# A graph network of four layers on one core: bf16 sums of weights in the first part of the last attention head, and one-time sums cut at the border of the head's parts

## The chip, the cores and the metric

The kernel runs on one core of a Trainium2 chip. The metric is the device time of that core in microseconds (us): the median of several executions. Times inside the kernel come from one further execution that the hardware profiler recorded.

## The reference

A graph of 2708 nodes has 512 features a node (`x`) and a symmetric 0/1 matrix `adj` with ones on the diagonal. Four layers are applied one after another, each as `x = x + L_i(relu(layernorm(x)), adj)`. L0 is a graph convolution, L1 a mean over the first 64 neighbours with two linear maps, L2 attention, L3 a sum over neighbours with two linear maps. The change lies in L2, which has 8 heads of 64 columns. For one head:

```python
Wh = h @ W[head]                       # 2708 x 64
e = leaky_relu(f1 + f2.T, 0.2)         # f1 = Wh @ a1, f2 = Wh @ a2: a number for each pair of nodes
att = softmax(where(adj > 0, e, -9e15), axis=1)
out = elu(att @ Wh)
```

## The kernel before, in words

**The trick of L2.** exp(leaky_relu(f1 + f2)) is the larger of two products, each of a factor of the row and a factor of the column. The kernel takes one factor out on each side, so that a tile of weights is the maximum of a row `rb` (the exponential of a row of numbers, the same in all partitions) and a number per partition `ec`, times the adjacency pattern `vT` of those nodes. The other number per partition, `ef`, is multiplied into the right operand. The softmax's denominator is the sum of the weights over the neighbours.

**Tiles and stages.** The neighbours (partitions) are cut into NC = 22 chunks of R = 126 nodes, the last of 62. The nodes that receive (columns) are whole, 2708 wide, for heads 1 to 6. For head 0 and head 7 they are cut in two parts at `cut` = 1384: units (lines 803 to 805) are head 0's two parts, heads 1 to 6, head 7's two parts: u = 0 to 9. Each unit has 22 steps, one per chunk (line 807), so there are 220 steps.

**One step.** `scale` (line 868, ScalarE) makes `whs`: the chunk's 64 columns of Wh times `ef` (line 874), and, where the sums need it, a block `one6` with a single column of ones times `ef` (line 876). `make` (line 880, VectorE, line 886) makes the tile of weights `t`, in one of four buffers. `multiply` (line 1077, TensorE) calls `four` (line 1065), whose matmuls (line 1069) each fill one of four groups of 32 columns of the array: `av`, the products of the weights with Wh in fp32, in pieces of the columns' halves, and `sums`, the weights' sums in fp32, in pieces of the columns' quarters. A part of 1384 columns has two pieces of 346 for `av` and one for `sums`; a whole head has three of some 451 and two of 338 and 339.

**Sums by side.** For some steps the fp32 pass for `sums` is replaced. `compare` (line 897, ScalarE, line 904) makes a 0/1 pattern `b` in bf16 that says for which neighbours the maximum was the row's number (a very steep sigmoid with the threshold in `eb`). `multiply_sides` (line 1092) multiplies this pattern in bf16 with `parts`, the factors split in three bf16 parts each, whose columns add up in the same PSUM buffers as the `sums` do. What does not depend on the pattern `b`, the sum over all neighbours of a factor of the partition, is the same for all such steps and is counted once at the start: `mask` (line 1138, ScalarE, line 1143) copies the adjacency of a chunk to bf16, a quarter of the columns at a time (677), and `count_neighbors` (line 1145, TensorE, line 1155) multiplies it with `parts2`, the split factors of all heads concerned, and after the last chunk stores the result to `sumT`. `split` (line 1117) makes `parts` and, with one copy (line 1132), `parts2`. Which steps go by side: chunks m with m mod 5 in 1, 3, 4, 13 of the 22 (BY_SIDE, line 795), in heads 1 to 6 (`by_side`, lines 809 and 810).

**What sets the order.** Each engine executes its instructions in the order in which the program issues them. The main loop (lines 1224 to 1239) issues for step s: the load of Wh for step s+6, scaling and making for s+3, comparing for s+1, multiplying for s, multiplying by side for s-1, and then what a plan holds for this step (`behind`, from line 1182): the split at step 9, the masks and the counting from step 11, the weights of layer 3 and `er` at step 30, evictions (`evict`, line 1102) at the end of each unit, the first steps of layer 3 in the last ones. In the built program some instructions stand elsewhere than in this loop, since a scheduler places them.

**Memory.** The pool `weights` (line 120) has two buffers of 8 KB a partition that all layers' weight matrices share, in order of use. The rows `a1` and `a2` lie in a pool of their own (line 915, loaded by `load_row`, line 176) and are read by `product2` (line 919). The pool `e3` (line 993) holds `er`, `rest` (scratch of `split`, and declared in line 995) and later `b3`, the bias of layer 3 (line 1246), which `self3` (line 1258) adds in line 1263. When `e3` is closed, the pool of layer 3's casts takes its place: `weight3` (line 1294) casts the pattern to `kt` in line 1296, for the matmuls in line 368. `load_l3_weights` (line 1177) loads `wfs` and `wfn`, layer 3's matrices.

Of the kernel before, what the change touches and what calls it, by code (L numbers as in the profile page):

```python
# [8 lines left out]
F32 = mybir.dt.float32  # L9
F32R = mybir.dt.float32r  # L10
BF16 = mybir.dt.bfloat16
# [9 lines left out]
P = 128  # L21

R = 126
# [21 lines left out]
def fast_layers(  # L45
# [36 lines left out]
    nc = tc.nc  # L82
    N, D = x_in.shape
    H, _, O = w2.shape
    NC = -(-N // R)
    NF = D // P
# [5 lines left out]
    def rows(c):  # L92
        return min(R, N - c * R)
# [26 lines left out]
    weights = ctx.enter_context(tc.tile_pool(name="weights", bufs=2))  # L120
    dram = ctx.enter_context(tc.tile_pool(name="dram", bufs=1, space=DRAM))

    common = ctx.enter_context(tc.tile_pool(name="common", bufs=2))

    ps = ctx.enter_context(tc.tile_pool(name="ps", bufs=8, space=PSUM, reuse_waits="tile"))
# [47 lines left out]
            nc.sync.dma_start(w[:, i], src[i * P : (i + 1) * P, :])  # L173
        return w

    def load_row(pool, src, name, tag=None):

        t = pool.tile([P, D], F32, name=name, tag=tag or name)
        nc.sync.dma_start(t, bass.AP(tensor=src.tensor, offset=src.offset, ap=[[0, P], [1, D]]))
        return t  # L180

# [107 lines left out]
    with tc.tile_pool(name="pre", bufs=2) as pre:  # L289
        ws = [load_weight(pre, w_self, "ws")]  # L290
        wc = load_weight(pre, w_comb, "wc", k=2 * NF)
        ws.append(load_weight(pre, w_nb3, "ws"))
        bc = load_row(pre, b_comb, "bc")
        bcol = pre.tile([P, 2 * NF], F32, name="bcol")
        for i, b in enumerate((b_self, b_nb3)):
# [51 lines left out]
    vT = []  # L347
# [69 lines left out]
    with ExitStack() as ring_ctx:  # L417
        ring = ring_ctx.enter_context(tc.tile_pool(name="ring", bufs=NC - 1, side="right"))
# [29 lines left out]
        with tc.tile_pool(name="l0", bufs=2) as wk:  # L448
            units = [(g, m) for g in range(len(groups)) for m in range(NC)]
# [191 lines left out]

        wk = ring_ctx.enter_context(tc.tile_pool(name="l1", bufs=1, side="right"))
        bl = load_row(wk, b_line1, "bl")
        bn = load_row(wk, b_nb1, "bn")
        wn, wl = l1_weights
        h1, turned = {}, {}
# [148 lines left out]
    BY_SIDE = [m for m in range(NC) if m % 5 in (1, 3, 4)]  # L795
# [6 lines left out]
    cut = EARLY * R // 8 * 8  # L802
    units = [(h, 0, N) for h in range(H)]
# [3 lines left out]
    steps = [(u, m) for u in range(len(units)) for m in range(NC)]  # L807

    def by_side(u, m):
        return 0 < units[u][0] < H - 1 and m in BY_SIDE  # L810

    whd = dram.tile([N, D], F32, name="whd")
    avT = dram.tile([D, N], F32, name="avT")
# [2 lines left out]
    sumT = dram.tile([NS, N], F32, name="sumT")  # L816
# [4 lines left out]
    at = at_ctx.enter_context(tc.tile_pool(name="att", bufs=1, reuse_waits="tile"))  # L821
# [3 lines left out]
    parts = at.tile([R, NC * H * 8 + S], BF16, name="parts")  # L825
    nc.gpsimd.memset(parts, 0.0)
    parts_of = parts[:, : NC * H * 8].rearrange("p (m h k) -> p m h k", h=H, k=8)
    parts2 = at.tile([R, NC, H, 3], BF16, name="parts2")
    nc.gpsimd.memset(parts2, 0.0)
    one6 = at.tile([R, S], F32, name="one6")  # L830
    nc.gpsimd.memset(one6, 0.0)
# [36 lines left out]
    def scale(s):  # L868

        u, m = steps[s]  # L870
        h, q = units[u][0], rows(m)
        t = at.tile([R, O + S], F32, name="whs", bufs=4)
        by = ef[:q, m, h : h + 1]
        ins = nc.scalar.activation(t[:q, :O], wh.pop((u, m))[:q], AF.Copy, scale=by)  # L874
        if not by_side(u, m):
            nc.scalar.activation(t[:q, O:], one6[:q], AF.Copy, scale=by)
        whs[s] = t
        scaled.append(ins.ins)
# [18 lines left out]
    def compare(s):  # L897

        u, m = steps[s]
        h, lo, hi = units[u]  # L900
        q = rows(m)
        if by_side(u, m):
            b = at.tile([R, N], BF16, name="b", bufs=2)
            nc.scalar.activation(  # L904
                b[:q, : hi - lo],
                weight[s][:q, : hi - lo],
                AF.Sigmoid,
                bias=eb[:q, m, h : h + 1],
                scale=STEEP,
            )  # L910
            sides[s] = b

    l2p = ctx.enter_context(ExitStack())
    pp = l2p.enter_context(tc.tile_pool(name="l2p", bufs=2, side="right", reuse_waits="tile"))
    ar = [load_row(pp, a, f"arow{i}") for i, a in enumerate((a1, a2))]

    products, firsts = {}, {}

# [73 lines left out]
    e3_ctx = ctx.enter_context(ExitStack())  # L992
    e3 = e3_ctx.enter_context(tc.tile_pool(name="e3", bufs=2, side="right", reuse_waits="tile"))
    er = e3.tile([R, NC, H], F32, name="er", bufs=1)
    rest = e3.tile([R, NC, H], F32, name="rest", bufs=1)
    kept3, l3_weights = {}, []


# [56 lines left out]
    def pieces(w):  # L1055

        k = -(-w // 512)
        cuts = [round(i * w / k) for i in range(k + 1)]
        return list(zip(cuts, cuts[1:]))
# [57 lines left out]
    def split():  # L1117

        nc.scalar.mul(eb, ec, -STEEP * ABOVE)
        for i in range(2):  # L1120
            e = ef
            if i:
                nc.vector.tensor_tensor(rest, ec, ef, ALU.mult)
                e = rest
            for k in range(3):
                part = parts_of[:, :, :, 3 * i + k]
                nc.scalar.copy(part, e)
                if k < 2:
                    nc.vector.tensor_tensor(rest, e, part, ALU.subtract)
                    e = rest  # L1130
        heads = slice(1, H - 1)
        nc.scalar.copy(parts2[:, :, heads], parts_of[:, :, heads, 3:6])


    quarter = N // 4
    counted, masks = [], {}

    def mask(i, j):
        m = BY_SIDE[i]
        q = rows(m)  # L1140
        g, k = where[m]
        t = masks[i, j] = common.tile([P, D], F32, name="x", bufs=XBUFS).bitcast(BF16)
        nc.scalar.copy(t[:q, :quarter], vT[g][:q, k, j * quarter : (j + 1) * quarter])

    def count_neighbors(i):
        m = BY_SIDE[i]
        q = rows(m)
        if i == 0:
            counted.extend(
                ps.tile([P, 512], F32, name="adj_sums", tag="ps") for _ in pieces(quarter)  # L1150
            )
        w = parts2[:q, m].rearrange("p h k -> p (h k)")
        for p, (a, b) in zip(counted, pieces(quarter)):
            for j in range(4):
                nc.tensor.matmul(
                    p[j * S : j * S + 3 * H, : b - a],
                    w,
                    masks[i, j][:q, a:b],
                    start=(i == 0),
                    stop=(i == len(BY_SIDE) - 1),  # L1160
                )
        if i < len(BY_SIDE) - 1:
            return
        for p, (a, b) in zip(counted, pieces(quarter)):
            t = common.tile([P, D], F32, name="out", tag="t", bufs=3)
            for j in range(4):
                own = slice(j * S, j * S + 3 * H)
                nc.scalar.copy(t[own, : b - a], p[own, : b - a])
                nc.sync.dma_start(
                    sumT[7 * H :, j * quarter + a : j * quarter + b], t[own, : b - a]  # L1170
                )

    def exp_nodes():
# [16 lines left out]
    behind(5, load_row1, *units[1])  # L1190
    behind(6, exp_row, *units[1])
    behind(9, split)
    behind(30, load_l3_weights)
    behind(30, exp_nodes)
# [8 lines left out]
    for i in range(len(BY_SIDE)):  # L1203
        for j in range(4):
            behind(11 + 2 * i + j // 2, mask, i, j)
        behind(13 + 2 * i, count_neighbors, i)
# [17 lines left out]
    for s in range(len(steps)):  # L1224
        if s + 6 < len(steps) and (s + 6) % NC % GROUP == 0:
            load_wh(s + 6)
        if s + 3 < len(steps):
            scale(s + 3)
            make(s + 3)
        if s + 1 < len(steps):  # L1230
            compare(s + 1)
        multiply(s)
        multiply_sides(s - 1)
        for fn, args in plan.pop(s, ()):
            if fn in (load_l3_weights, exp_nodes, split):
                with tc.issue_after(made[s]):
                    fn(*args)
            else:
                fn(*args)
# [3 lines left out]

    with ExitStack() as stack:
        ring = stack.enter_context(tc.tile_pool(name="ring3", bufs=NC - 1, reuse_waits="tile"))
        b3 = e3.tile([P, D], F32, name="b3", bufs=1)
        nc.sync.dma_start(
            b3, bass.AP(tensor=bias3.tensor, offset=bias3.offset, ap=[[0, P], [1, D]])
        )
# [688 lines left out]
def kernel(tc: tile.TileContext, *args: bass.AP):  # L1938

    nc = tc.nc  # L1940
    with tc.tile_pool(name="verdict", bufs=1) as pool:
        verdict = pool.tile([1, 1], I32, name="verdict")
        fast_layers(tc, *args, verdict)
        odd = nc.values_load(verdict[0:1, 0:1], min_val=0, max_val=P + 1)
        with tc.If(odd > 0):
            general_layers(tc, *args)
# [32 lines left out]
```

## Time and profile before

| | us |
|---|---|
| median of 3 runs | 1822.22 |
| lowest, highest | 1820.46, 1822.46 |
| profiled execution | 1820.7 |
| its span | 1818.8 |
| TensorE busy in it | 1781.6 |
| VectorE busy | 1307.9 |
| ScalarE busy | 798.0 |
| all matmuls of line 1069, `av` | 436.2 |
| all fp32 matmuls of line 1069, `sums` | 139.6 |

The profile gives for each engine its busy time, the groups of instructions by line with the mean duration of one, and what ended the idle time before them. The chain of waits follows the work that ended last back to its start; it says which engine sets the time in a stretch. A timeline lists what an engine did, with equal instructions in a row joined (x16 is sixteen of them). PE is TensorE, DVE is VectorE, ACT is ScalarE, POOL is GpSimd, SP is SyncE, which only issues transfers. The mean TensorE clock granted over the span was 0.996 of full speed. Attention's steps run from about 853 to 1411 us, unit 8 from 1330.5 to 1369, and layer 3's sum over the neighbours from 1589.7.

### The profile page before, as it was taken

The numbers are of one execution on the slowest core, as the hardware profiler recorded it, in microseconds if no ns is written. First come the engines' busy times: TensorE is split into PE (matmuls) and PEld (weight loads), VectorE is DVE, ScalarE is ACT, GpSimd is POOL, SyncE is SP. The second block draws the span as 40 slices with busy tenths as digits, with TensorE's granted clock in tenths as the row PEclk, the third lists the DMA queues.
The fourth block names the chain that finished last, engine by engine and source line by source line (L and its number), as shares of the span: only waits on it lengthen the run. The fifth ranks groups of instructions, "written<-read, shape, count | busy, mean of one in ns | idle before, by whom it ended". The sixth has DMA issues, their size and how long they took to land.

```text
span 1818.8 us, 30698 instructions
## 1 busy us (share of the span) xinstructions
PE 1781.6 (98%) x11884; PEld 1036.1 (57%) x11884; DVE 1307.9 (72%) x1836; ACT 798.0 (44%) x1542; POOL 245.3 (13%) x241
## 2 busy tenths in 40 slices
PE   9899999999999999999999999999999999999998
PEld 4456777654447887644444344444444454488776
DVE  4942998955546655888999999999998777533334
ACT  2642777722110000156887767767744566400000
POOL 0101333301121111266000000000001222100000
PEclk9999999999999999999999999999999999999999
DMA  7632666635461211343221121122022444313221
GB/s 248 193 114 67 204 208 196 204 76 121 117 149 55 67 54 46 97 147 104 73 61 26 42 62 43 27 61 57 13 65 56 134 131 139 94 38 102 78 69 45
DMA packets 165554, 176.63 MB, mean 97 GB/s; under 512 B 94830, under 2 KB 115792, under 8 KB 164516
## 3 DMA queue, kind: packets, MB, share of 16 engines
q1 hardware_dynamic: 143170, 131.47, 26.2%
q10 hardware_dynamic: 18484, 33.28, 5.4%
q0 software_dynamic: 3744, 9.82, 1.6%
q8 instruction: 96, 1.57, 0.4%
q14 instruction: 60, 0.49, 0.1%
HBM read 111.35 MB, written 55.15 MB: 92 GB/s over the span
## 4 chain that ended last, share of the span: by engine, by line
PE 80%; DVE 9%; issue 4%; DMA 4%; ACT 1%; POOL 1%; SPq 0%; DVEq 0%; ACTq 0%; POOLq 0%
PE acc L368 31%; PE av L1069 19%; PE nb_ps L184 7%; PE sums L1069 6%; PE self_ps L184 4%; PE wh_ps L184 3%; DVE t L886 3%; PE line_ps L184 3%; DVE cum L494 2%; PE h_ps L184 2%; PE hT_ps L212 2%; PE fused_ps L312 2%; DMA x<-x 1%; DMA ai<-in_adj 1%; DVE two L506 1%
## 5 line engine op out<-in xcount | busy, mean ns | idle before, releaser
L886 DVE SCALAR_TENSOR_TENSOR t<-rb,ec,vT 126x2708 f32<-126x2708 f32 (+2 forms) x220 | 532.2, 2472 | 17.6 <-PE sums L1069 9.7
L368 PE MATMUL acc<-halves,kt 126*126 126x512 f32 x1848 | 435.9, 395 | 3.9 <-DVE kt L741 2.3
L1069 PE MATMUL av<-t,whs 126*32 126x451 f32 (+3 forms) x4576 | 436.2, 515 | 0.6 <-DVE ln_mv L191 0.6
L368 PEld LDWEIGHTS acc<-halves,kt 126*126 126x126 f32 x1848 | 342.6, 186 | 93.7 <-DVE kt L741 6.9
L1069 PEld LDWEIGHTS av<-t,whs 126*32 126x32 f32 (+1 forms) x4576 | 158.7, 110 | 207.8 <-issue 188.0
L368 PE MATMUL acc<-halves,ar 126*126 126x512 f32 x924 | 232.7, 405 | 2.1 <-DVE deg L502 1.1
L904 ACT ACTIVATE b<-t,eb 126x2708 bf16<-126x2708 f32 (+1 forms) x78 | 199.1, 2552 | 25.4 <-DVE t L886 25.1
L368 PEld LDWEIGHTS acc<-halves,ar 126*126 126x126 f32 x924 | 169.1, 186 | 52.7 <-issue 7.7
L193 ACT ACTIVATE ln_rs<-ln_mv,eps 126x1 f32<-126x1 f32 x88 | 25.6, 293 | 339.5 <-DVE ln_mv L191 336.5
L741 DVE SCALAR_TENSOR_TENSOR kt<-lastr,index,vT 126x504 fp32r<-126x504 int16 (+3 forms) x154 | 110.6, 729 | 81.0 <-PE acc L368 80.7
L1296 DVE CAST kt<-vT 126x504 fp32r<-126x504 uint8 (+3 forms) x154 | 56.0, 366 | 138.2 <-PE acc L368 138.2
L1069 PE MATMUL sums<-t,whs 126*32 126x338 f32 (+5 forms) x1568 | 139.6, 449 | 2.4 <-ACT out L1110 2.4
L874 ACT ACTIVATE whs<-wh,ef 126x64 f32<-126x64 f32 x220 | 76.8, 349 | 130.6 <-PE sums L1069 66.1
L1036 POOL TENSOR_SCALAR z<-y 126x512 f32<-126x512 f32 x22 | 44.0, 2000 | 662.2 <-DVE y L1029 653.4
L494 DVE TENSOR_TENSOR_SCAN cum<-ai,deg 126x504 int16<-126x504 int32 (+2 forms) x110 | 128.6, 1182 | 0.5 <-DMA ai<-in_adj 0.5
L522 ACT ACTIVATE cum<-cum,limit 126x504 int16<-126x504 int16 (+3 forms) x132 | 88.2, 668 | 58.4 <-DVE deg L502 57.3
L1069 PEld LDWEIGHTS sums<-t,whs 126*32 126x32 f32 (+1 forms) x1568 | 54.9, 109 | 70.0 <-issue 43.7
L189 DVE BATCH_NORM_STATS2 ln_st<-x 126x6 f32<-126x512 f32 x88 | 60.4, 686 | 43.1 <-DMA x<-x 29.1
L184 PE MATMUL h_ps<-w0s,hT 128*126 128x512 f32 x176 | 79.7, 596 | 6.0 <-ACT hT L214 4.7
L184 PE MATMUL nb_ps<-wfn,hT 128*126 128x512 f32 x176 | 81.7, 608 | 2.0 <-ACT hT L214 2.0
L184 PE MATMUL wh_ps<-w2s,hT 128*126 128x512 f32 (+1 forms) x176 | 79.4, 593 | 0.0
L184 PE MATMUL nb_ps<-wn,hT 128*126 128x512 f32 x176 | 79.2, 592 | 0.0
(182 smaller groups left out, 1869.8 us busy)
## 6 DMA issues: line engine op xcount, KB each, us to landing
x<-x SPq DMA_DIRECT2D x105, 252.0 KB
x<-x ACTq DMA_DIRECT2D x84, 252.0 KB
ai<-in_adj SPq DMA_DIRECT2D x84, 249.0 KB
x<-in_x SPq DMA_DIRECT2D x42, 252.0 KB
rb<-rT SPq DMA_DIRECT2D x7, 1332.8 KB
wh<-whd SPq DMA_DIRECT2D x70, 94.5 KB
packed<-two POOLq DMA_DIRECT2D x44, 124.5 KB, 4.3
whd<-wh SPq DMA_DIRECT2D x21, 252.0 KB
```

The lines of the kernel that those rows point to most:

```text
L184: nc.tensor.matmul(po[:n], lhsT[:, f, :n], w[:, f, :], start=(f == 0), stop=(f == NF - 1))
L189: nc.vector.bn_stats(st[:n], xc[:n])
L368: nc.tensor.matmul(acc[:R], weight[:, k * R : (k + 1) * R], parts[:, i, :], start=(m == 0 and i == 0), stop=(m == NC - 1),)
L494: nc.vector.tensor_tensor_scan(cum[:n, :gw], ai[:n, :gw], ai[:n, :gw], 0.0 if g == 0 else deg[:n, m : m + 1], op0=ALU.add, op1=ALU.max,)
L522: nc.scalar.activation(cum[:n, :gw], cum[:n, :gw], AF.Sign, bias=limit[:n], scale=-1.0, accum_out=signs[:n, m, g : g + 1],)
L741: nc.vector.scalar_tensor_tensor(by_chunk(kt, cs), lastr[:, cs[0] * R : (cs[-1] + 1) * R].rearrange("p (c r) -> p c r", r=R), index[:R, m ...
L874: ins = nc.scalar.activation(t[:q, :O], wh.pop((u, m))[:q], AF.Copy, scale=by)
L886: ins = nc.vector.scalar_tensor_tensor(t[:q, : hi - lo], row[h][:q, lo:hi], ec[:q, m, h : h + 1], vT[g][:q, k, lo:hi], op0=ALU.max, op1=AL ...
L904: nc.scalar.activation(b[:q, : hi - lo], weight[s][:q, : hi - lo], AF.Sigmoid, bias=eb[:q, m, h : h + 1], scale=STEEP,)
L1036: nc.gpsimd.tensor_scalar(z, y, 0.0, None, op0=ALU.min)
L1069: nc.tensor.matmul(p[j * S : (j + 1) * S, : b - a], lhsT, rhs[:, part * size + a : part * size + b], start=(s % NC == 0), stop=(s % NC == ...
L1296: nc.vector.tensor_copy(by_chunk(kt, cs), pattern(m, cs))
```

## The change

1. `by_side` takes unit 8, head 7's first part, in too. Its 13 steps of BY_SIDE get a comparison and a bf16 pass in place of a scaling of `one6` and an fp32 pass.
2. The one-time sums are cut at 0, 692, 1384, 2046 and 2708 instead of in quarters of 677, so that no piece crosses the border between head 7's parts. `parts2` holds two sets of factors for each of the 13 chunks: with head 7 for the first two fourths, without it for the others. `split` fills it with six copies instead of one.
3. Three things move in memory: the rows `a1` and `a2` into a buffer of the pool `weights`, `rest` to the pool `common`, `b3` to the pool `ring3`.

```diff
     def by_side(u, m):
-        return 0 < units[u][0] < H - 1 and m in BY_SIDE
+        return 1 < u < len(units) - 1 and m in BY_SIDE
...
-    parts2 = at.tile([R, NC, H, 3], BF16, name="parts2")
+    parts2 = at.tile([R, len(BY_SIDE), 2, H, 3], BF16, name="parts2")
...
-    ar = [load_row(pp, a, f"arow{i}") for i, a in enumerate((a1, a2))]
+    arows = weights.tile([P, NF, D], F32, name="arows", tag="w")
+    ar = [load_row(None, a, None, into=arows[:, i]) for i, a in enumerate((a1, a2))]
...
-    rest = e3.tile([R, NC, H], F32, name="rest", bufs=1)
...
     def split():
...
+        rest = common.tile([P, D], F32, name="rest", tag="t", bufs=3)
+        rest = rest[:R, : NC * H].rearrange("p (m h) -> p m h", h=H)
...
-        heads = slice(1, H - 1)
-        nc.scalar.copy(parts2[:, :, heads], parts_of[:, :, heads, 3:6])
-    quarter = N // 4
+        for i, heads in enumerate((slice(1, H), slice(1, H - 1))):
+            for r in sorted({m % 5 for m in BY_SIDE}):
+                ms = [m for m in BY_SIDE if m % 5 == r]
+                src = parts_of[:, r :: 5, heads, 3:6]
+                at_i = [BY_SIDE.index(m) for m in ms]
+                nc.scalar.copy(parts2[:, at_i[0] : at_i[-1] + 1 : 3, i, heads], src)
+    fourths = [0, cut // 2, cut, (cut + N) // 2, N]
...
-        nc.scalar.copy(t[:q, :quarter], vT[g][:q, k, j * quarter : (j + 1) * quarter])
+        nc.scalar.copy(t[:q, : own.stop - own.start], vT[g][:q, k, own])
...
-        for p, (a, b) in zip(counted, pieces(quarter)):
+        for n, p in enumerate(counted):
             for j in range(4):
+                a, b = pieces_of(j)[n]
                 nc.tensor.matmul(
                     p[j * S : j * S + 3 * H, : b - a],
-                    w,
+                    parts2[:q, i, j // 2].rearrange("p h k -> p (h k)"),
                     masks[i, j][:q, a:b],
...
-        b3 = e3.tile([P, D], F32, name="b3", bufs=1)
+        b3 = ring.tile([P, D], F32, name="b3", bufs=1)
```

In the order of instructions of the changed program, beside the above: on SP's queue the two rows are loaded where `wfs` was, `wfs` where `wfn` was, `wfn` behind it and one load of `wh`, and `b3` behind the last stores of the sums; on VectorE the first three casts of line 1296 stand ahead of the last normalization and the last three additions of line 1263, behind which they stood before. The comparison for the second step of unit 8 stands on ScalarE ahead of unit 7's evictions.

More of the change, by code (lines that the diff above doesn't have):

```diff
@@ L174, in load_weight, with load_row @@
         return w
-    def load_row(pool, src, name, tag=None):
-        t = pool.tile([P, D], F32, name=name, tag=tag or name)
+    def load_row(pool, src, name, into=None):
+        t = into
+        if t is None:
+            t = pool.tile([P, D], F32, name=name)
         nc.sync.dma_start(t, bass.AP(tensor=src.tensor, offset=src.offset, ap=[[0, P], [1, D]]))
@@ L1130, in split, with pieces_of @@
                     e = rest
-        heads = slice(1, H - 1)
-        nc.scalar.copy(parts2[:, :, heads], parts_of[:, :, heads, 3:6])
-    quarter = N // 4
+        for i, heads in enumerate((slice(1, H), slice(1, H - 1))):
[5 more added lines that the diff above has]
+    fourths = [0, cut // 2, cut, (cut + N) // 2, N]
     counted, masks = [], {}
+    def pieces_of(j):
+        return pieces(fourths[j + 1] - fourths[j])
     def mask(i, j):
@@ L1141, in mask @@
         g, k = where[m]
+        own = slice(fourths[j], fourths[j + 1])
         t = masks[i, j] = common.tile([P, D], F32, name="x", bufs=XBUFS).bitcast(BF16)
-        nc.scalar.copy(t[:q, :quarter], vT[g][:q, k, j * quarter : (j + 1) * quarter])
+        nc.scalar.copy(t[:q, : own.stop - own.start], vT[g][:q, k, own])
     def count_neighbors(i):
@@ L1149, in count_neighbors @@
             counted.extend(
-                ps.tile([P, 512], F32, name="adj_sums", tag="ps") for _ in pieces(quarter)
+                ps.tile([P, 512], F32, name="adj_sums", tag="ps") for _ in pieces_of(0)
             )
-        w = parts2[:q, m].rearrange("p h k -> p (h k)")
-        for p, (a, b) in zip(counted, pieces(quarter)):
+        for n, p in enumerate(counted):
             for j in range(4):
+                a, b = pieces_of(j)[n]
                 nc.tensor.matmul(
                     p[j * S : j * S + 3 * H, : b - a],
-                    w,
+                    parts2[:q, i, j // 2].rearrange("p h k -> p (h k)"),
                     masks[i, j][:q, a:b],
@@ L1163, in count_neighbors @@
             return
-        for p, (a, b) in zip(counted, pieces(quarter)):
+        for n, p in enumerate(counted):
             t = common.tile([P, D], F32, name="out", tag="t", bufs=3)
             for j in range(4):
+                a, b = pieces_of(j)[n]
                 own = slice(j * S, j * S + 3 * H)
@@ L1169, in count_neighbors @@
                 nc.sync.dma_start(
-                    sumT[7 * H :, j * quarter + a : j * quarter + b], t[own, : b - a]
+                    sumT[7 * H :, fourths[j] + a : fourths[j] + b], t[own, : b - a]
                 )
```

## The prediction

> **What bounds the kernel now.** I read the busy shares first, then the chain of work that ended last, then the timelines of TensorE, VectorE and ScalarE in the stretches that the edits touch.
>
> ```profile
> PE 1781.6 (98%) x11884; PEld 1036.1 (57%) x11884; DVE 1307.9 (72%) x1836; ACT 798.0 (44%) x1542; POOL 245.3 (13%) x241
> PE 80%; DVE 9%; issue 4%; DMA 4%; ACT 1%; POOL 1%; SPq 0%; DVEq 0%; ACTq 0%; POOLq 0%
> ```
>
> TensorE (PE) is busy 98% of the span and is 80% of the chain. A microsecond of matmul taken out is a microsecond won, unless the next engine in that stage is late. So I look at the stage: unit 8, head 7's first part, from 1330.5 to 1369 us. The chain of waits there holds nothing but PE (start, us, what):
>
> ```profile
> 1334.56 1.17 PE av L1069 x16
> 1335.72 0.58 PE sums L1069 x8
> 1336.31 1.17 PE av L1069 x16
> 1337.47 0.58 PE sums L1069 x8
> ```
>
> A step is 1.17 + 0.58 = 1.75 us (the starts of `av` are 1.75 apart). `av` is two pieces of 346 columns by four column groups in fp32, `sums` one such piece. The groups show what is to take the place of `sums`, and what the other engines would have to deliver (busy us, mean ns of one, idle before):
>
> ```profile
> L1069 PE MATMUL sums<-t,whs 126*32 126x346 f32 x336 | 32.1, 453 | 0.0
> L1069 PE MATMUL sums<-b,parts 126*32 126x338 bf16 x288 | 25.0, 306 | 0.0
> L886 DVE SCALAR_TENSOR_TENSOR t<-rb,ec,vT 126x1384 f32<-126x1384 f32 x42 | 69.1, 1659 | 7.8 <-ACT rb L849 2.6 <-PE sums L1069 2.5 <-PE av L1069 1.1
> L904 ACT ACTIVATE b<-t,eb 126x2708 bf16<-126x2708 f32 x72 | 183.7, 2552 | 23.6 <-DVE t L886 23.2 <-ACT whs L874 0.2
> ```
>
> The mean ns of a matmul includes its pipeline and overlaps its neighbours' (453 against 306 understates the difference), so I take starts. In a whole head, a bf16 pass has two pieces, of 338 and 339 columns, and moves the next `av` by 0.29 us (1311.16 to 1311.45, in the timeline). One piece of 346 is then 0.146 x 346/338.5 = 0.15 us.
>
> VectorE is idle only about 0.1 us in each step: it waits for a buffer that PE releases (four buffers of `t`). ScalarE rests in most of each step (start, us, in brackets the idle before):
>
> ```profile
> 1339.91 0.35 ACT L874 ACTIVATE whs<-wh,ef 126x64 f32<-126x64 f32 x1 [1.18 <-issue]
> 1340.17 0.31 ACT L876 ACTIVATE whs<-one,ef 126x32 f32<-126x32 f32 x1
> 1341.67 0.35 ACT L874 ACTIVATE whs<-wh,ef 126x64 f32<-126x64 f32 x1 [1.20 <-PE sums L1069]
> ```
>
> Two other places matter. At the start of layer 3's sum over neighbours PE stands 1.39 us for a cast that VectorE does behind the last `y`:
>
> ```profile
> 1589.73 2.55 PE L368 MATMUL acc<-halves,kt 126*126 126x512 f32 x10 [1.39 <-DVE kt L1296]
> 1588.37 0.68 DVE L1263 TENSOR_TENSOR y<-self_ps,b 62x512 f32<-62x512 f32 x1 [2.12 <-PE self_ps L184]
> 1589.17 1.07 DVE L1296 CAST kt<-vT 126x504 fp32r<-126x504 uint8 x3
> ```
>
> And at the end of attention PE idles 0.60 and 1.83 us, and then runs at half clock for two windows (1409.65 to 1416.48):
>
> ```profile
> 1407.71 0.62 PE L212 MATMUL hT_ps<-ident,hn 126*128 126x126 f32 x4 [1.83 <-DVE hn L203]
> 1411.63 6.09 PE L184 MATMUL nb_ps<-wfn,hT 128*126 128x512 f32 x8
> ```
>
> **What the Trainium skill says.** "FP8 and Floating Point Precision", section TensorE Precision Notes: true fp32 takes four passes through the array. The trace agrees: 0.58 us against 0.15 is a ratio of 3.9. "ScalarE: Activation LUTs", section What ACT_TABLE_LOAD costs: an activation with a per-partition bias takes about 280 ns plus 0.833 ns an element, whatever the function; L904 at 2708 columns would be 2.54, and 2.552 was measured. "TensorE: Matmul & The Clock Gate", section What's actually happening: too little work in a window of 3413 ns halves the clock, and the window runs free. The trace has just such windows at 1409.65. "DMA: Bandwidth & Descriptors", section Issuing engines are not separate DMA queues: loads of all queues share the same 16 engines. So moved loads must be looked at for what they land beside.
>
> **The change, part by part.**
>
> *Unit 8's sums.* 13 of its 22 steps (m mod 5 in 1, 3, 4) lose the fp32 pass (0.58) and get a bf16 one (0.15), one step later in PE's order: 13 x 0.43 = 5.6 us less on PE. Unit 8 goes from 22 x 1.75 = 38.5 to 9 x 1.75 + 13 x 1.32 = 32.9. Can the others follow?
> - VectorE must make 22 tiles. One has a duration of 1.66, but in a run where it waits for nothing they start 1.57 apart (1321.78, 1323.35): 34.5 us, 1.6 more than PE. It enters unit 8 with its four buffers full: a tile is ready about 3.3 us before PE takes it. 3.3 - 1.6 leaves 1.7 at the end (1.3 when I step through the order with the buffer releases). Unit 9 stays as it is (PE 1.68, VectorE 1.51 a step), so the lead grows back by 0.17 a step. If tiles came 1.66 apart, VectorE would need 36.5, 0.3 us more than PE and lead together; counting release delays I put the gain then at 3.8.
> - ScalarE gets 13 compares in place of 13 scalings of `one6` (0.31 each). The trace has no compare of 1384 columns. Bounds: 1.36, the exponential of that width on the same engine (next of kin, without a bias operand), and 2.55, a whole-width compare. I take 1.43: 0.28 + 0.833 x 1.384 by the page, and 2.552 less 1324 columns at 0.836 (the slope of L849 from 1384 to 2708) is 1.44. Work in unit 8, without waits: 9 x 0.56 + 13 x (0.25 + 1.43 - 0.09 of overlap) + 2.4 for unit 7's evictions = 28.1 (9.5 + 13 compares), under PE's 32.9. It would reach 32.9 at a compare of 1.80 and 38.5 at 2.23.
> - The compare stands ahead of unit 7's evictions (`out<-av`), which then come up to 1.4 us later. Units 7 and 8 together hold 5 + 3 of the eight PSUM buffers, and unit 9 needs its own only 30 us on: free.
> - The unseen cost is the bf16 pass in steps this short: 0.15 at best, 0.30 (a whole pass's time) at worst: gain 5.6 to 3.6. I take 5.6.
>
> *One-time sums in fourths.* 104 mask copies keep their total width (692 + 692 + 662 + 662 = 2708), 104 matmuls too: 26 pieces are wider by some 8 columns, below 0.1 us each way. One copy of `parts2` (0.54) becomes six of 84 to 105 elements, each about the 0.25 to 0.29 of L876: some 1.1 us more on ScalarE between 876.8 and 880.6, where it idles 0.34 + 1.19 us. Cost 0; if that cover is gone, PE waits up to 1 us more for the masks, for which it already waits 0.9 us in all. The memset on GpSimd grows from 528 to 624 elements, far ahead of its use.
>
> *Moved buffers and loads.* The two `a` rows go into a weight buffer, so on SP's queue they take the place of `wfs` at 545 us, `wfs` takes that of `wfn` (from 853.8), and `wfn`, 1 MB, comes behind it, waiting for the last product that reads the rows (about 856.5, before SP arrives there). Behind these four on SP stand `er` and the group of `wh` issued at 864.1, which is needed at 868.4. At 0.82 us an issue, `wfn` takes SP from 858.2 to 861.5 and lands by about 864, since 1 MB takes near 4 us at the 277 GB/s seen here: a slack of some 2 us stays. Cost 0; up to 2 us if it were used up. `b3` no longer lies in the buffer pool of `rest` and `er`; its load goes from 858.3 to behind the last sums' stores, at 1414 in the times of before, ahead of the next `aT`, `sT` and `x`. It is first read at 1422.0, 8 us later; the page gives 4.3 us to landing for a load of half its size, so some 3 us are left. Cost 0, at worst 1.
>
> *Layer 3's first casts.* As `b3` left that pool, the pool's next owner, `kt`, no longer waits for the last reader of `b3`. VectorE's order in the changed program has the first three casts before the last norm and the last three `y`. VectorE has idle stretches of 0.8 to 3.4 us there, and the delayed norm has 4 us of slack. The 1.39 us go; next late is nothing, since `halves` are ready.
>
> Sum: -5.6 - 1.4 + 0.1 = -6.9 us on the profiled execution's 1820.7: 1813.8. The median is 1822.2, 1.5 more, and I move it alike: **1815.3**.
>
> **The rivals.**
> 1. *VectorE or the short pass sets unit 8's pace in part*: -3.7 - 1.4, 1817.1. For it: VectorE's total is above PE's. Against it: the lead.
> 2. *The casts' wait is replaced*, by the next operand or by a colder clock: -5.6 alone, 1816.7. PE's clock and the last `y` there speak for it.
> 3. *The windows at the end of attention move.* Half clock for 6.8 us costs about 3.5 us; the earlier end gives another phase. Both ways alike: 1811.8 or 1818.8.
> 4. *Unit 8 doesn't get faster at all*, VectorE being held by its buffers, which now wait for ScalarE's reading too: -1.4, 1820.8.
> 5. *Slower: ScalarE becomes the bound of unit 8.* If the compare does not shrink with its width (2.55), ScalarE needs 9.5 + 13 x 2.55 = 42.7 against 38.5 before, and 13 waits from engine to engine, of the 0.1 us that VectorE shows, make it 44.0: +5.5 - 1.4 = +4.1, 1826.3. It costs from 2.23 us a compare on, and outweighs the casts' 1.4 from 2.34. Against it: the exponential of 1384 columns took 1.36.
>
> **How the numbers follow.** Chances: my forecast 0.54 (1813.3 to 1817.3); rival 1 0.12; rival 2 0.11; rival 3 0.05 each way; rival 4 0.07; rival 5 0.06. A measurement of this kernel can tell some 0.2%, 3.6 us, from no change: faster is below 1818.6, slower above 1825.9. Faster: 0.54 + 0.12 + 0.11 + 0.05 = 0.82; same: 0.05 + 0.07 = 0.12; slower 0.06. The range takes in both sides of rival 3 and leaves out rivals 4 and 5 (0.13): 1811.4 to 1819.2.
>
> **What would show it.** In unit 8 the chain should be PE alone, with steps of 1.32 and 1.75 us in the pattern of m; compares of 1.4 us on ScalarE; VectorE's makes without idle time. PE's wait for `kt` should be gone, and that for masks stay under 2 us. A wait of PE for `t` or `b` in unit 8, a compare over 1.8 us, a wait for `b3` or `wh`, or new half-clock windows would make it wrong.

## The result, and the profile after

| | before | after |
|---|---|---|
| median of 20 runs, us | 1822.34 | 1815.67 |
| lowest, highest | 1818.29, 1825.81 | 1810.58, 1821.78 |
| profiled execution's span | 1818.8 | 1811.3 |

The ratio is 0.9965, with a 95% interval of 0.9956 to 0.9974: the changed kernel is faster by 6.4 us (4.7 to 8.0 by the interval). The forecast was 1815.3.

The line of busy times of the page after, first:

```profile
PE 1773.1 (98%) x11832; PEld 1043.1 (58%) x11832; DVE 1306.6 (72%) x1836; ACT 813.6 (45%) x1547; POOL 245.0 (14%) x241
```

TensorE has 8.5 us less to do, ScalarE 15.6 more, VectorE nearly the same (1.3 less). The chain of waits in unit 8, after (start, us, what):

```profile
1338.49 1.17 PE av L1072 x16
1339.66 0.73 PE sums L1072 x12
1340.38 2.33 PE av L1072 x32
1342.72 0.73 PE sums L1072 x12
```

It is still PE alone. 0.73 is an fp32 pass (0.58) followed by a bf16 one of the step before (0.15). 2.33 is the `av` of two steps with no fp32 pass between them. Five steps, two of 1.75 and three of 1.31, repeat every 7.43 us: `av` of such a group starts at 1338.31 and again at 1345.74 in the timeline. The groups, after, by shape:

```profile
L1072 PE MATMUL sums<-t,whs 126*32 126x346 f32 x240 | 22.9, 453 | 0.0
L1072 PE MATMUL sums<-b,parts 126*32 126x346 bf16 x48 | 4.0, 310 | 0.0
L889 DVE SCALAR_TENSOR_TENSOR t<-rb,ec,vT 126x1384 f32<-126x1384 f32 x42 | 67.7, 1653 | 5.9 <-ACT rb L852 2.7 <-PE sums L1072 1.8 <-PE av L1072 1.1
L907 ACT ACTIVATE b<-t,eb 126x1384 bf16<-126x1384 f32 x12 | 17.3, 1440 | 1.6 <-DVE t L889 1.5
```

Of the records of fp32 `sums` of 346 columns 96 are gone, 8 for each of 12 full chunks; 48 in bf16 have come, 4 each (the 13th chunk has 62 rows and its own groups). The compare of 1384 columns takes 1.440 us. VectorE's timeline shows the stage in one line, 36 makes from 1332.48 on with no gap above 0.11 us between them:

```profile
1332.48 57.13 DVE L889 SCALAR_TENSOR_TENSOR t<-rb,ec,vT 126x1384 f32<-126x1384 f32 x36 [0.15 <-PE sums L1072]
```

Layer 3's start on PE, in its timeline:

```profile
1579.06 3.60 PE L186 MATMUL self_ps<-wfs,hT 128*126 128x512 f32 x8
1582.09 8.24 PE L370 MATMUL acc<-halves,kt 126*126 126x512 f32 x33
```

No bracket stands behind the first `acc`: the wait of 1.39 us for `kt` is gone. From the last `nb_ps` to the first `acc` it is now 3.46 us instead of 5.42. In VectorE's timeline the first casts now stand 16 us ahead of the last `y`:

```profile
1566.49 0.41 DVE L1310 CAST kt<-vT 126x504 fp32r<-126x504 uint8 x1
...
1582.70 0.68 DVE L1277 TENSOR_TENSOR y<-self_ps,b 62x512 f32<-62x512 f32 x1 [2.12 <-PE self_ps L186]
```

To see where the time went, I cut the profiled executions at four matmuls: the last `av` of the last chunk of units 7 and 8, the first `nb_ps` of layer 3 and the last one. The end is that of PE's last matmul, some 7.5 us ahead of the span's end. Times in us:

| | to unit 7's end | unit 8 | to first nb_ps | to last nb_ps | to the end | sum |
|---|---|---|---|---|---|---|
| before | 1328.10 | 38.76 | 44.77 | 172.68 | 226.92 | 1811.23 |
| after | 1329.99 | 33.54 | 43.62 | 171.48 | 225.27 | 1803.90 |
| difference | +1.89 | -5.22 | -1.15 | -1.20 | -1.65 | -7.33 |
| no_u8 | 1328.56 | 38.76 | 45.77 | 173.30 | 225.31 | 1811.70 |
| b3_only | 1328.64 | 38.76 | 44.63 | 172.82 | 225.26 | 1810.11 |
| u8_no_moves | 1331.09 | 33.54 | 44.42 | 172.91 | 226.90 | 1808.86 |

Two columns take only two values each: unit 8 is 38.76 or 33.54, the last column 226.9 or 225.3. The others vary between executions by some us whatever the kernel. The three kernels below the differences are experiments.

### The profile page after: what moved, and what is told of

It is laid out like the page before. It is cut to its first block, busy times and chain, and to the rows that moved or that the text cites. A ratio compares the mean times of both kernels' runs of the same rounds, so it can differ in the third digit from the quotient of the medians.

```text
span 1811.3 us, 30604 instructions
## 1 busy us (share of the span) xinstructions
PE 1773.1 (98%) x11832; PEld 1043.1 (58%) x11832; DVE 1306.6 (72%) x1836; ACT 813.6 (45%) x1547; POOL 245.0 (14%) x241
## 4 chain that ended last, share of the span: by engine, by line
PE 83%; DVE 9%; DMA 3%; issue 3%; ACT 1%; POOL 1%; SPq 0%; DVEq 0%; ACTq 0%; POOLq 0%
PE acc L370 32%; PE av L1072 19%; PE nb_ps L186 8%; PE sums L1072 6%; PE self_ps L186 4%; PE line_ps L186 4%; PE wh_ps L186 3%; DVE t L889 3%; PE h_ps L186 2%; DVE cum L496 2%; PE hT_ps L214 2%; PE fused_ps L314 2%; DMA ai<-in_adj 1%; DVE two L508 1%; DMA x<-in_x 1%
## 5 line engine op out<-in xcount | busy, mean ns | idle before, releaser
L1072 PEld LDWEIGHTS av<-t,whs 126*32 126x32 f32 (+1 forms) x4576 | 164.9, 110 | 198.8 <-issue 173.8
L907 ACT ACTIVATE b<-t,eb 126x2708 bf16<-126x2708 f32 (+3 forms) x91 | 217.8, 2393 | 35.6 <-DVE t L889 34.0
L1072 PE MATMUL sums<-t,whs 126*32 126x338 f32 (+4 forms) x1464 | 129.9, 447 | 2.4 <-ACT out L1113 2.4
```

The source lines that it names most:

```text
L907: nc.scalar.activation(b[:q, : hi - lo], weight[s][:q, : hi - lo], AF.Sigmoid, bias=eb[:q, m, h : h + 1], scale=STEEP,)
L1072: nc.tensor.matmul(p[j * S : (j + 1) * S, : b - a], lhsT, rhs[:, part * size + a : part * size + b], start=(s % NC == 0), stop=(s % NC == ...
```

## The experiments

My theory was that the gain has two sources that add up: TensorE's shorter passes in unit 8, and the wait for `kt` that went when `b3` changed its pool. The rivals were that the loads and buffers moved brought it, or that only the whole does.

**Unit 8 left alone** (no_u8), the rest of the change kept:

```diff
-        return 1 < u < len(units) - 1 and m in BY_SIDE
+        return 1 < u < len(units) - 2 and m in BY_SIDE
...
-        for i, heads in enumerate((slice(1, H), slice(1, H - 1))):
+        for i, heads in enumerate((slice(1, H - 1), slice(1, H - 1))):
```

> The changed kernel with unit 8 left as it was before (fp32 sums in all its steps; the second set of factors then serves all fourths, and the moved buffers stay). Theory (the bf16 pass is worth 5.6 us, the earlier casts 1.4): unit 8 takes 38.5 us again, PE does not wait for kt at the start of layer 3, and the time is 1820.9, a ratio of 0.9992 to the kernel before. Rival (the gain came from the moved buffers and loads): it stays near 1816, a ratio of 0.9965.

Measured: 0.9989 (0.9980 to 0.9997), 1819.81. Unit 8 took 38.76 us, and the last stretch is as short as after the change. The rival's 0.9965 lies outside the interval.

**Only b3 moved** (b3_only), in the kernel before:

```diff
-        b3 = e3.tile([P, D], F32, name="b3", bufs=1)
+        b3 = ring.tile([P, D], F32, name="b3", bufs=1)
```

> The kernel before with one edit: b3 in the pool ring3. Theory: the first three casts come ahead of the last y, PE's wait of 1.39 us for kt goes, nothing else moves: from the last neighbour product (last nb_ps) to layer 3's first acc 3.5 us instead of 5.4, the time 1820.9, a ratio of 0.9992. Rival (another wait takes its place, or the casts need the other moves): 5.4 us there and a ratio of 1.0000.

Measured: 0.9985 (0.9978 to 0.9992), 1819.26. PE goes over to `acc` without a wait:

```profile
1585.28 3.60 PE L184 MATMUL self_ps<-wfs,hT 128*126 128x512 f32 x8
1588.31 4.07 PE L368 MATMUL acc<-halves,kt 126*126 126x512 f32 x15
```

So this one line is enough; the rows and `rest` have nothing to do with it.

**Unit 8 without the moves** (u8_no_moves): the changed kernel with the rows, `rest` and `b3` in their old places.

```diff
-    arows = weights.tile([P, NF, D], F32, name="arows", tag="w")
-    ar = [load_row(None, a, None, into=arows[:, i]) for i, a in enumerate((a1, a2))]
+    ar = [load_row(pp, a, f"arow{i}") for i, a in enumerate((a1, a2))]
...
+    rest0 = e3.tile([R, NC, H], F32, name="rest", bufs=1)
...
-        rest = common.tile([P, D], F32, name="rest", tag="t", bufs=3)
-        rest = rest[:R, : NC * H].rearrange("p (m h) -> p m h", h=H)
+        rest = rest0
...
-        b3 = ring.tile([P, D], F32, name="b3", bufs=1)
+        b3 = e3.tile([P, D], F32, name="b3", bufs=1)
```

> The changed kernel with the three memory moves undone: unit 8 by side and one-time sums in fourths, but the rows a1 and a2, rest and b3 where they were. Theory: unit 8 takes 33 us instead of 38.5, the wait of 1.39 us for kt stays, the time is 1816.7, a ratio of 0.9969. Rival (the edits help only together): 1820 or more.

Measured: 0.9972 (0.9965 to 0.9980), 1815.42. Unit 8 is at 33.54 us, and the old wait stands where it stood:

```profile
1587.38 2.81 PE L370 MATMUL acc<-halves,kt 126*126 126x512 f32 x11 [1.39 <-DVE kt L1309]
```

In the three ratios the parts are 0.0028 for unit 8 and 0.0011 to 0.0015 for the casts; their sum, 0.0039 to 0.0043, goes with 0.0035 for both, within the intervals.

**How near are the other engines?** Three kernels put more work into unit 8 to find from which point ScalarE or VectorE would have taken the gain; the unedited changed kernel ran beside them.

act_400 and act_twice follow each compare of unit 8 by a second one that writes the same values, over 400 columns and over all 1384:

```diff
+            if u == 8:
+                nc.scalar.activation(
+                    b[:q, :400],
+                    weight[s][:q, :400],
+                    AF.Sigmoid,
+                    bias=eb[:q, m, h : h + 1],
+                    scale=STEEP,
+                )
             sides[s] = b
```

> The changed kernel with each compare of unit 8 followed by a second one over its first 400 columns (the same values again). It adds 13 x 0.52 us to ScalarE's work there (0.28 + 400 x 0.00083, less 0.09 of overlap), which is 28.2 by my sum. Theory (ScalarE decides from 1.80 us a compare on; this is 1.96): ScalarE needs 9.5 + 13 x 1.96 = 35.0, unit 8 takes 35 us instead of 33.5, the time is 1817.2. Rival (ScalarE has more room than that): 33.5 and 1815.7. Second rival (waits from engine to engine come on top): 37 or more.

> The changed kernel with each compare of unit 8 done twice (the same values again), as if it cost 1.44 + 1.34 = 2.78 us. Theory: ScalarE is the bound, unit 8 takes 9.5 + 13 x 2.78 = 45.6 us instead of 33.5, the time is 1827.8, slower than the kernel before (ratio 1.0030). Rival (the queues between the engines hide part of it): below 41 us in unit 8 and no slower than before.

Measured: act_400 0.9958 (0.9944 to 0.9972), act_twice 0.9993 (0.9984 to 1.0002). The engines' busy times in unit 8, in columns as the view of stretches has them (stretch, its length, PE, PEld, DVE, ACT, POOL, PE's clock, DMA share, GB/s), for after, act_400 and act_twice:

```profile
1329.99:1363.53 33.54, 33.54 (x487) 15.18 (x480) 32.58 (x21) 27.00 (x50) 0.00 (x0) 1.00 0.31 82
```

```profile
1328.83:1362.37 33.54, 33.54 (x488) 15.16 (x480) 32.58 (x21) 32.13 (x60) 0.00 (x0) 1.00 0.30 82
```

```profile
1330.53:1368.81 38.28, 36.03 (x483) 15.24 (x476) 33.18 (x21) 38.28 (x55) 0.00 (x0) 1.00 0.26 72
```

With 5 us more on ScalarE nothing changes: the rival was right there, and my expectation of 35 wrong. ScalarE does work 34.1 us from the first of these compares to the end of the last, more than the stretch has, but it begins 1.6 us ahead of it. With the compare doubled the rival was right too: the median is 1819.37 where I expected 1827.8. ScalarE is then busy without a pause and is the bound, but unit 8 takes 38.28 us, not 45.6. The work itself was estimated well: in ScalarE's timeline it goes on from the first compare at 1328.96 to the end of the last at 1373.0, 44 us. But it begins 1.6 us before the stretch and ends 4.2 us after it:

```profile
1328.96 1.43 ACT L907 ACTIVATE b<-t,eb 126x1384 bf16<-126x1384 f32 x1
...
1371.56 1.45 ACT L915 ACTIVATE b<-t,eb 62x1384 bf16<-62x1384 f32 x1
```

A compare is issued one step ahead of its chunk's `av` and its pass comes one step later, so ScalarE may drift from first to last without holding PE all the time. Not all of this room was there in the changed kernel. In the built program of act_twice the last passes stand later in PE's order: that of chunk 21 comes behind the `av` of unit 9's third chunk, and in the changed kernel behind the `sums` of its first (PE's timelines, after and act_twice):

```profile
1365.05 0.74 PE L1072 MATMUL sums<-t,whs 126*32 126x331 f32 x8
1365.72 0.33 PE L1072 MATMUL sums<-b,parts 62*32 62x346 bf16 x4
```

```profile
1370.48 0.74 PE L1080 MATMUL sums<-t,whs 126*32 126x331 f32 x8
1371.04 1.30 PE L1080 MATMUL av<-t,whs 126*32 126x331 f32 x16
1372.15 0.73 PE L1080 MATMUL sums<-t,whs 126*32 126x331 f32 x8
1372.71 1.28 PE L1080 MATMUL av<-t,whs 126*32 126x331 f32 x10
1373.92 0.33 PE L1080 MATMUL sums<-b,parts 62*32 62x346 bf16 x4
```

How much of the room is due to this order no run tells; in act_400 the order is that of the changed kernel. Of the 4.7 us that unit 8 takes longer, the view of waits names 1.8 as waits for these compares, in three places. Unit 9's last chunk starts 80.8 us after unit 7's end against 75.4.

dve_128 follows each make of unit 8 by a second one over its first 128 columns, with the same values:

```diff
         )
+        if u == 8:
+            ins = nc.vector.scalar_tensor_tensor(
+                t[:q, :128],
+                row[h][:q, lo : lo + 128],
+                ec[:q, m, h : h + 1],
+                vT[g][:q, k, lo : lo + 128],
+                op0=ALU.max,
+                op1=ALU.mult,
+            )
         weight[s] = t
```

> The changed kernel with each make of unit 8 followed by a second one over its first 128 columns (the same values again): VectorE gets 22 x 0.26 = 5.7 us more there and needs 40.1. Theory (the lead of 3.3 us covers what VectorE lacks, and no more): unit 8 takes 40.1 - 3.3 = 36.8 us instead of 33.5, and unit 9 and layer 3's first chunk lose 1 to 2 more since the lead is gone: the time is 1820.0 to 1821.3. Rival A (TensorE alone sets the pace): 33.5 in unit 8, 1815.7. Rival B (VectorE already set the pace): 39.2 in unit 8.

Measured: 0.9999 (0.9990 to 1.0007), 1821.87. Unit 8 took 38.59 us, 1.8 more than the theory and 0.6 less than rival B. It is 5.05 us longer than in the changed kernel, and the median is 6.6 us above that of the changed kernel beside it, for 5.7 us of added work. The view of waits names part of PE's waits (us in total, times, longest):

```profile
PE av L1081 <- DVE t L898: 2.4, 5, 1.0
```

One thing spoils the number: from chunk 6 on, the built program does two makes and then their two additions, so that the first tile of a pair is ready one make (1.57 us) later than it would be alone. That is about the 1.8 us missing, but I didn't run it in another order. What follows safely is that this much more work on VectorE, in this order, is paid for almost in full. That VectorE already set the pace of the changed kernel (rival B) doesn't follow: there PE is busy for all of unit 8's 33.54 us.

> The changed kernel once more, unedited, beside the three: 1815.7, unit 8 in 33.5 us.

Measured: 0.9966 (0.9952 to 0.9980), 1815.31, unit 8 in 33.54 us.

**A version that beats both.** Unit 9 is left. u9_too takes it in:

```diff
-        return 1 < u < len(units) - 1 and m in BY_SIDE
+        return 1 < u and m in BY_SIDE
...
-        for i, heads in enumerate((slice(1, H), slice(1, H - 1))):
+        for i, heads in enumerate((slice(1, H), slice(1, H))):
...
         multiply_sides(s - 1)
+        if s == len(steps) - 1:
+            multiply_sides(s)
```

> The changed kernel with unit 9, head 7's second part, by side as well (both sets of factors then hold head 7, and the last step's pass comes at its own end). TensorE loses another 13 x 0.42 = 5.5 us of matmuls. Theory (VectorE is the next bound): in the two units together VectorE was busy 72.8 of 77.2 us after the change, so at most 4 us can be won, and I expect 1 to 3: about 1813.7, a ratio of 0.9953. Rival (TensorE alone counts): 1810.2, a ratio of 0.9934. A second rival (VectorE, out of its lead, is late in layer 3's first chunk): no gain on the changed kernel, 0.9965.

Measured: 0.9942 (0.9928 to 0.9956), 1809.87. The interval holds both the theory's 0.9953 and the first rival's 0.9934, so the time doesn't decide between them. The trace shows a wait that neither named. Counted from unit 7's end, PE is through the fp32 pass of unit 9's chunk 20 after 67.7 us, 4.6 earlier than after the change (72.4), and then stands (PE's timeline):

```profile
1399.58 0.33 PE L1072 MATMUL sums<-b,parts 126*32 126x331 bf16 x4 [2.18 <-ACT b L907]
1399.84 1.88 PE L1072 MATMUL av<-t,whs 62*32 62x331 f32 x16
1401.48 0.51 PE L1072 MATMUL sums<-b,parts 62*32 62x331 bf16 x4
1403.67 1.07 PE L214 MATMUL hT_ps<-ident,hn 126*128 126x126 f32 x4 [1.68 <-DVE hn L205]
```

At the first `nb_ps` only 1.1 us of the 4.6 are left (76.05 against 77.16). ScalarE's timeline shows why: the last two compares, and a load of the table for their function, stand ahead of the norm:

```profile
1396.84 1.28 ACT L907 ACT_TABLE_LOAD   x1
1398.13 1.40 ACT L907 ACTIVATE b<-t,eb 126x1324 bf16<-126x1324 f32 x1
...
1399.66 1.40 ACT L907 ACTIVATE b<-t,eb 62x1324 bf16<-62x1324 f32 x1
1401.08 1.28 ACT L195 ACT_TABLE_LOAD   x1
1402.37 0.29 ACT L195 ACTIVATE ln_rs<-ln_mv,eps 126x1 f32<-126x1 f32 x1
```

A second gain lies behind the first `nb_ps`, and it isn't one of matmuls taken out. In the changed kernel PE waits 3.21 us (before the change 2.02) ahead of the second chunk's `nb_ps`. ScalarE's copy of `hT` stands there behind an activation `th`, which waits for GpSimd (PE's and ScalarE's timelines, after):

```profile
1418.54 3.70 PE L186 MATMUL nb_ps<-wfn,hT 128*126 128x512 f32 x8 [3.21 <-ACT hT L216]
```

```profile
1416.72 0.63 ACT L1042 ACTIVATE th<-z 126x512 f32<-126x512 f32 x1 [2.60 <-POOL z L1039]
1417.38 0.63 ACT L1043 ACTIVATE z<-z 126x512 f32<-126x512 f32 x1
1417.91 0.57 ACT L216 ACTIVATE hT<-hT_ps 128x504 f32<-128x504 f32 x1
```

In the built program of u9_too the copy stands ahead of that activation, and PE waits 0.68 us:

```profile
1414.61 0.59 ACT L216 ACTIVATE hT<-hT_ps 128x504 f32<-128x504 f32 x1 [1.23 <-PE hT_ps L214]
1415.22 1.28 ACT L1042 ACT_TABLE_LOAD   x1
1416.52 0.63 ACT L1042 ACTIVATE th<-z 126x512 f32<-126x512 f32 x1
```

From the first `nb_ps` to the second chunk's it is 9.54 us there against 11.39. No run changed this order alone, so what unit 9's passes brought by themselves is not shown.

To have the norm earlier, u9_part leaves chunks 19 and 21 of unit 9 in fp32 (the edit is against the changed kernel):

```diff
-        return 1 < u < len(units) - 1 and m in BY_SIDE
+        return 1 < u and m in BY_SIDE and (u < len(units) - 1 or m < 19)
...
-        for i, heads in enumerate((slice(1, H), slice(1, H - 1))):
+        for i, end in enumerate((NC, 19)):
+            heads = slice(1, H)
...
-                ms = [m for m in BY_SIDE if m % 5 == r]
-                src = parts_of[:, r :: 5, heads, 3:6]
+                ms = [m for m in BY_SIDE if m % 5 == r and m < end]
+                src = parts_of[:, r:end:5, heads, 3:6]
...
+        late = slice(1, H - 1)
+        nc.scalar.copy(parts2[:, 11:13, 1, late], parts_of[:, 19:22:2, late, 3:6])
```

> The changed kernel with unit 9 by side as well, but only for chunks below 19 (11 of its 22 steps; the second set of factors then leaves head 7 out for chunks 19 and 21). In u9_too PE waited 2.18 us for the last compare, and ScalarE's last two compares, 1.4 us each, and a load of 1.28 for their function stood ahead of the norm (ln_rs) that layer 3's first products wait for. Theory: without them hn of chunk 0 comes 2 us earlier, the two fp32 passes (0.8 us) lie beside that wait, and the first nb_ps comes about 49.5 us after unit 7's last chunk... instead of 76.05 in u9_too, 74 to 74.5; the time is 1808.3, a ratio of 0.9932 to the kernel before. Rival (VectorE's chain of layer 3's first chunk is the bound there): 76, and no difference from u9_too (0.9942).

> The same kernel as u9_too, unedited, beside u9_part on one chip: 1809.9, a ratio of 0.9942; from unit 7's last chunk to the first nb_ps 76 us.

(The 49.5 in the first text is a slip; the stretch meant is the 76.05 us.) Measured: u9_part 0.9926 (0.9913 to 0.9940), 1807.49; u9_too once more 0.9942 (0.9928 to 0.9956), 1810.08. The stretch from unit 7's end to the first `nb_ps` is 72.8 us in u9_part, where 74 to 74.5 was expected, and 76.1 in u9_too. ScalarE's norm now comes 1.6 us earlier, at 1400.75, although this execution reached unit 7's end 1.3 us later:

```profile
1397.98 0.30 ACT L879 ACTIVATE whs<-one,ef 62x32 f32<-62x32 f32 x1
...
1399.46 1.28 ACT L195 ACT_TABLE_LOAD   x1 [1.17 <-DVE rs L1030]
1400.75 0.29 ACT L195 ACTIVATE ln_rs<-ln_mv,eps 126x1 f32<-126x1 f32 x1
```

Some 0.4 us of the 3.3 is the clock's: u9_too's two profiles have a half-clock stretch from 1400.5 and 1401.1 on, u9_part's has none there, and from `hT_ps` to `nb_ps` the first of them takes 2.04 us and u9_part 1.62. The rest is more than expected, and why stays open. The copy of `hT` stands early in u9_part too (from the first `nb_ps` to the second chunk's it is 9.31 us), so some 2 us of its gain on the changed kernel go with that order. u9_part does less by side than u9_too and has the lowest median measured here; the intervals of the two overlap.

## Why the prediction was right, point by point

*Unit 8's sums, 5.6 us.* Right, and the trace agrees closely: the stretch in the table ends at the last chunk's `av`, ahead of the 13th pass, so 12 x 0.435 = 5.22 us are to be seen in it, and are. Of the 13th, 0.2 us is seen: from unit 8's end to unit 9's last chunk it is 41.8 us instead of 42.0. The rest of the 1.15 us in the next column is before's half-clock stretch.

*VectorE follows.* Right. Its last tile was ready at 1361.1 and was taken at about 1362.6: a lead of 1.5 us at the end, where 1.3 to 1.7 was predicted. dve_128 shows that this was the narrow point: with 5.7 us more on VectorE, the time is that of the kernel before (0.9999). Rivals 1 and 4 described a kernel not far from this one: each had VectorE hold back unit 8.

*ScalarE's compare, 1.43 us.* Right in its size (1.440) and in ScalarE's sum (27.0 busy against 28.1). Wrong in the threshold: I let ScalarE decide from a compare of 1.80 us on, and rival 5 be slower than before from 2.34. At 1.96 nothing was lost, and at 2.78 the kernel as a whole was still level with the one before (0.9993). The step that failed is the sum of ScalarE's work against PE's time in the same unit: I granted VectorE its lead and gave ScalarE none. 9.5 + 13 x 2.78 is 45.6, 38.28 was measured, 7.3 less: 5.8 of them is ScalarE's drift past both ends of the stretch, the rest work that was reckoned too high. On this count PE would be reached at about (33.5 + 7.3 - 9.5) / 13 = 2.4 us a compare. That last number is an estimate and not measured, and it rests on the order of passes in act_twice.

*One-time sums in fourths, 0.1 us or nothing.* Right. The six copies take 1.08 us together, twice the one before, and ScalarE idles 1.06 before the masks:

```profile
879.53 1.08 ACT L1141 COPY parts<-parts 126x105 bf16<-126x105 bf16 x6
...
882.79 0.35 ACT L877 ACTIVATE whs<-wh,ef 126x64 f32<-126x64 f32 x1 [1.06 <-PE sums L1072]
883.05 0.30 ACT L879 ACTIVATE whs<-one,ef 126x32 f32<-126x32 f32 x1
883.26 2.04 ACT L1156 CAST x<-vT 126x692 bf16<-126x692 uint8 x3
```

The masks start 26.90 us after attention's first `av` in both kernels (880.59 - 853.69, 883.26 - 856.36), and PE waits 0.9 us for them in both.

*Moved loads, nothing.* Right. Everything on SP's queue that follows `wfn` is issued 2.67 us later than before, and so is the whole stage (its first `av` at 856.36 against 853.69), so nothing is late. (In after_again's profile the first `av` stands at 853.92: the 2.67 us are one execution's.) `b3` is issued at 1410.88 and first read at 1416.28, without a wait.

*Layer 3's first casts, 1.4 us.* Right: the wait of 1.39 us is gone, nothing takes its place, and b3_only shows that it is this move that does it. The stretch from the last `nb_ps` to the end is shorter by 1.65, in all three kernels with `b3` moved alike. Up to the first `acc` 1.96 is won, since matmuls that follow without a pause also overlap by some 0.57 in the records, and 0.3 is lost again behind it.

*Half-clock windows, both ways alike.* In the profile of before there are two at the end of attention, one behind the other, in that after none. They are worth 0.95 us between unit 9's last chunk and the first `nb_ps`. The first eight `nb_ps` matmuls took 6.09 us in the one and 3.70 in the other, and 1.19 of these 2.39 us came back as the longer wait for `hT` behind them (3.21 against 2.02), which leaves the 1.20 us of the table. So some 2.1 of the 7.33 us in the table are the clock's. The +1.89 us ahead of unit 8 isn't the change's either: the same changed kernel, in after_again's profile, reached unit 7's end at 1328.30, 0.20 behind before. That two such amounts nearly cancel in the profiles is luck. The medians don't rest on it: the mean granted clock was 0.9956 over the changed kernel's 20 runs, and 0.9960 over 47 runs of the kernel before beside the first experiments.

## What to carry to other kernels

When a step is moved off a full engine, draw up the account of each other engine in that stage alone, and give every engine its own lead or lag: how many steps ahead of its consumer it is issued, and how many buffers stand between. A queue that may drift can be short of time in a stage and cost nothing, as ScalarE in act_400, or less than it lacks, as in act_twice; one with 1.5 us left, as VectorE, is used up by the next edit. And look for waits that come from memory, not from data: a bias in the pool that the next stage reuses held back that stage's first casts, and one line freed them.

## What the runs showed of the hardware that was not expected

- Inside the span the TensorE clock was halved in stretches of 3.41 or 6.83 us, not at the same places in each execution of the same kernel: in the changed kernel's profile at 396.2, in its second profile at 78.5, 1006.9 and 1416.5. Some places recur: from 1006.2 to 1008.6 in eight of the twelve profiles, at the end of attention in ten. The two in the midst of before, 1006.9 and 1409.7, each follow a stretch of 3.41 us in which PE was busy only 1.14 and 1.94 us. Both profiles of the changed kernel have a span of 1811.3, yet such a stretch costs time: with the one at 1416.5 the way from the second chunk's `nb_ps` to the third's took 9.52 us instead of 8.02, and that execution had been 1.7 us ahead at unit 7's end.
- Six copies of some 100 elements took 1.08 us together, 0.18 each, where I had priced each at 0.25 to 0.29 from single short activations.
